# Layer 0 of a four-layer convolution and attention network: a written order for its convolutions, one tile of x kept in SBUF, batch norms of q, k and v apart, attention's first image begun earlier

## The chip, the cores and the metric

The kernel runs on one core of a Trainium2 chip. The core has five engines with queues of their own: TensorE (PE, with its weight loads listed as PEld), VectorE (DVE), ScalarE (ACT), GpSimd (POOL) and SyncE (SP), which here only issues DMAs. The metric is the device time of one execution in microseconds (us), lower is better.

## The reference, cut to what matters

x has the shape (8, 384, 32, 32), float32. Four layers each add their output to x. The change lies in layer 0:

```python
def _dwproj(x, dw, g, b, pw):                     # for q, k and v, with weights of their own
    y = conv(x, dw, 3x3, padding 1, depthwise)    # 384 channels
    y = gelu(_bn(y, g, b))                        # batch norm over (image, h, w), per channel
    return einsum('oc,bchw->bohw', pw, y)
...
q, k, v = (_dwproj(gn(x), ...) per heads of 48 channels)
attn = softmax(einsum('bhcn,bhcm->bhnm', q, k) * scale)
out = einsum('oc,bchw->bohw', w_out, attn @ v)
x = x + _bn(out)
```

gn is a group norm of x per image (32 groups of 12 channels). The batch norm of q, say, needs the mean and variance of q's convolution over all eight images, so no gelu of q can run before all of q's convolutions are done. The other layers (a mixture of four experts, a 7x7 depthwise convolution, a fusion of three branches) aren't touched.

## The kernel before

The 384 channels are three tiles of 128 partitions, ct = 0, 1, 2; an image has N = 1024 pixels. Layer 0 has these stages.

**Statistics** (L237 to L246). Each image of x is loaded whole (1.5 MB, SP, L241, four buffers), DVE takes its statistics (bn_stats, L140, bn_aggr, L245), and `gn_coefs` turns these into a scale and a shift per channel and image (s0, t0).

**Inputs** (`prepare`, L252 to L264). For one ct, each image's 128 channels are loaded again (0.5 MB, SP, L259, tile xn, three buffers), normalized by ACT (`affine`, L200) and transposed in 32x32 blocks by DVE (L261) into xt0, where 32 channels x 32 rows lie so that a convolution along a row is a banded 32x32 matrix. xt0 has two buffers. POOL clears its border rows.

**Convolutions** (`convolve0`, L266 to L292). For each (ct, v), v = q, k, v, a block of four groups u. A group loads a weight tile (0.4 MB, on ACT's queue, L271, four buffers), runs 96 matmuls of the source, 192 in the trace, on 32x32 pieces of PE (L278) into one of two PSUM buffers of four banks, and ACT copies the buffer into the tile o (L284, two buffers of o). After four groups, DVE transposes each image back into y (L290, four buffers), takes the batch norm's statistics (L140), and SP writes y to DRAM (raw[v][b], L292). I call the last three the results of a block.

The order here is that of the source as a scheduler arranges it: `prepare(0)`, `prepare(1)`, the blocks (0, q), (0, k), (0, v), then `prepare(2)`, then the six others. After the last block `bn_coefs` (L203 to L210) computes scale and shift of all nine (v, ct) at once: bn_aggr on DVE, a power on POOL (L135), and three small products.

**Attention** (`attention(False)`). From here the order on PE, ACT and DVE is that of the source (`manual_schedule`); SP and POOL are arranged by the scheduler, in order of the source as a rule. For each image, `fetch` loads q, k and v (1.5 MB each, L364), `activate` applies batch norm and gelu on ACT (three affines of 128x1024, L200), `project_k` and `project_q` multiply by pw_k and pw_q (36 matmuls of the trace each, L380, into three PSUM buffers of two banks, evicted by ACT and by DVE copies, L398 and L400), `scores` multiplies q by k (L472) and takes exp on ACT (L479), `project_v` (L425) makes v, `attend` (L491) multiplies. For the first image the order is: fetch(0), gelu of k, gelu of q, project_k, gelu of v, project_q, scores, project_v. `attention(True)` is a second version that runs only if a sum left the range of float32; it is skipped with these inputs.

After the batch norms, and before attention in the source, w1 (2.3 MB, the experts' weights of layer 1), gate_w and gate_b are loaded on SP.

Of the kernel before, what the change touches and what calls it, by code (L numbers as in the profile page):

```python
# [17 lines left out]
P = 128  # L18
# [49 lines left out]
def img(a):  # L68
    return a.rearrange("p (h w) -> p h w", w=W)
# [3 lines left out]
def conv_mixer_kernel(ctx: ExitStack, tc: tile.TileContext, a: dict, out: bass.AP):  # L73
# [63 lines left out]
    def bn_stats_of(bs, src):  # L137

        for h in range(2):
            nc.vector.bn_stats(bs[:, h, :], src[:, h * HF : (h + 1) * HF])  # L140
# [58 lines left out]
    def affine(o, i, s, t, func=AF.Identity):  # L199
        nc.scalar.activation(o, i, func, bias=t, scale=s)  # L200

    def bn_coefs(stats, gb, n, s, t):

        mv = small.tile([P, 2, 9], FP, tag="bn_mv", name="bn_mv")
        for i in range(n):
            nc.vector.bn_aggr(mv[:, :, i], stats[:, i].rearrange("p a s -> p (a s)"))
        rsqrt(s, mv[:, 1, :n])
        nc.vector.tensor_mul(s, s, gb[:, :, 0])
        nc.vector.tensor_mul(t, mv[:, 0, :n], s)
        nc.vector.tensor_sub(t, gb[:, :, 1], t)  # L210
# [19 lines left out]
        for v in range(3)  # L230
    ]

    with tc.tile_pool(name="cw", bufs=1) as cw, tc.tile_pool(name="cxt", bufs=2) as cxt:
        bn_gb = load(cw, "bn_gb", nc.scalar)
        stats = cw.tile([P, 9, 2 * B, 6], FP, name="stats")
        with tc.tile_pool(name="cx", bufs=4) as cx, tc.tile_pool(
            name="cgn", bufs=2, space=PSUM  # L237
        ) as cgn:
            for b in range(B):
                x = cx.tile([P, NC, N], FP, tag="x", name="x")  # L240
                nc.sync.dma_start(out=x, in_=a["x"][b])  # L241
                for ct in range(NC):
                    bs = xst[:, ct, 2 * b : 2 * b + 2, :]
                    bn_stats_of(bs, x[:, ct, :])
                    nc.vector.bn_aggr(mvx[:, :, ct, b], bs.rearrange("p a s -> p (a s)"))  # L245
            s0, t0 = gn_coefs((mvx[:, 0], mvx[:, 1]), cgn)  # L246

        with tc.tile_pool(name="co", bufs=2, reuse_waits="tile") as co, tc.tile_pool(
            name="cy", bufs=3, reuse_waits="tile"
        ) as cy, tc.tile_pool(name="cps", bufs=2, space=PSUM, reuse_waits="tile") as cps:  # L250

            def prepare(ct):  # L252

                xt = cxt.tile([P, 32, B, H + 2], FP, tag="xt0", name="xt0")
                for row in (0, H + 1):
                    nc.gpsimd.memset(xt[:, :, :, row : row + 1], 0.0)
                for b in range(B):
                    xn = cy.tile([P, N], FP, tag="xn", name="xn")
                    nc.sync.dma_start(out=xn, in_=a["x"][b, :, ct, :])  # L259
                    affine(xn, xn, s0[:, ct, b : b + 1], t0[:, ct, b : b + 1])  # L260
                    nc.vector.transpose(  # L261
                        xt[:, :, b, 1 : 1 + H].rearrange("p c h -> p h c"), img(xn)
                    )
                return xt  # L264

            def convolve0(ct, v, xt):  # L266

                o = co.tile([P, B, H, 32], FP, tag="o", name="o")
                for u in range(4):
                    w = cy.tile([P, 2, 4, 3, W], FP, tag="w", name="w", bufs=4)  # L270
                    nc.scalar.dma_start(out=w, in_=a["w0"][ct, v, u])  # L271
                    ps = cps.tile([P, 4, 2, B, H], FP, tag="ps", name="ps")
                    for cc in range(2):
                        for k in range(3):
                            for j in range(4):
                                for i in range(4):
                                    r = slice(32 * i, 32 * i + 32)
                                    nc.tensor.matmul(  # L278
                                        ps[32 * j : 32 * j + 32, i, cc],
                                        lhsT=w[r, cc, j, k, :],  # L280
                                        rhs=xt[r, 8 * j + 2 * u + cc, :, k : k + H],
                                        start=k == 0, stop=k == 2,
                                    )
                    nc.scalar.copy(  # L284
                        o.rearrange("p b h (i c) -> p i c (b h)", i=4)[:, :, 2 * u : 2 * u + 2],
                        ps.rearrange("p i c b h -> p i c (b h)"),
                    )
                for b in range(B):
                    y = cy.tile([P, N], FP, tag="y", name="y", bufs=4)
                    nc.vector.transpose(img(y), o[:, b])  # L290
                    bn_stats_of(stats[:, v * NC + ct, 2 * b : 2 * b + 2, :], y)
                    nc.sync.dma_start(out=raw[v][b][:, ct, :], in_=y)  # L292

            xts = [prepare(0), prepare(1)]
            for ct in range(NC):
                for v in range(3):
                    convolve0(ct, v, xts[ct])
                    if (ct, v) == (0, 2):
                        xts.append(prepare(2))
        bn_coefs(stats, bn_gb, 9, bn_s, bn_t)  # L300


    zraw = [dram.tile([P, NC, N], FP, tag=f"z{b}", name=f"z{b}") for b in range(B)]
    wpool = ExitStack()
    wp = wpool.enter_context(tc.tile_pool(name="wp", bufs=1))
    w1 = load(wp, "w1")
    gate_w = load(wp, "gate_w")
    gate_b = load(wp, "gate_b")
    zpool = ExitStack()
    zs = zpool.enter_context(tc.tile_pool(name="zs", bufs=1))  # L310
    zst = zs.tile([P, NC, 2 * B, 6], FP, name="zst")
# [6 lines left out]
    def attention(shifted):  # L318
# [3 lines left out]
        with tc.tile_pool(name="aw", reuse_waits="tile", bufs=1) as aw, tc.tile_pool(  # L322
# [5 lines left out]
            w_out = load(aw, "w_out")  # L328
            if shifted:

                pw_q, pw_k = load(aw, "pw_qs"), load(aw, "pw_ks")
                ones_row = aw.tile([P, 1], FP, name="ones_row")
                nc.gpsimd.memset(ones_row, 0.0)
                nc.gpsimd.memset(ones_row[0:1, :], 1.0)
                nc.gpsimd.memset(ones_row[64:65, :], 1.0)
            else:
                pw_q, pw_k = load(aw, "pw_q"), load(aw, "pw_k")

                own = aw.tile([P, 3], FP, name="own")
                nc.gpsimd.memset(own, 1.0)
                for o, base, sign in ((1, 15, -1), (2, -16, 1)):
                    for q in range(4):
                        v = own[32 * q : 32 * q + 32, o : o + 1]
                        nc.gpsimd.affine_select(
                            out=v, in_=v, compare_op=ALU.is_ge, fill=0.0, base=base,
                            pattern=[[0, 1]], channel_multiplier=sign,
                        )
                nc.gpsimd.tensor_copy(own[32:64, 0:1], own[32:64, 1:2])  # L350
                nc.gpsimd.tensor_copy(own[64:96, 0:1], own[64:96, 2:3])
# [1 line left out]
            nc.gpsimd.memset(vT, 1.0)  # L353
            chk = aw.tile([P, B * 2 * NP], FP, name="chk")
            if shifted:
                mx = aw.tile([P, 4, P], FP, name="mx")
                nc.gpsimd.memset(mx, 0.0)
            ys, kTs, qTs, atts, xs = {}, {}, {}, {}, {}

            def fetch(b):  # L360
                ys[b] = []
                for v in range(3):
                    y = ay.tile([P, NC, N], FP, tag=f"y{v}", name=f"y{v}", bufs=1)
                    nc.sync.dma_start(out=y, in_=raw[v][b])  # L364
                    ys[b].append(y)

# [181 lines left out]
            ]  # L548
            per_b = len(todo) // B
            fetch(0)  # L550
            activate(0, 1)
            last = None
            for i, t in enumerate(todo):
                b, j = t[0], i % per_b
                if j == 0:
                    activate(b, 0)
                    project_k(b)
                    activate(b, 2)
                    project_q(b)
                    if shifted:  # L560
                        shift(b)
                es = scores(*t)
                complete = attend(*last) if last else None
                if j == 0:
                    project_v(b)
                    if b + 1 < B:
                        fetch(b + 1)
                if complete:
                    complete()
                last = (*t, es)  # L570
                if j == 3 and b > 0:
                    project_out(b - 1, 1)
                if j == per_b // 2 + 3:
                    if b + 1 < B:
                        activate(b + 1, 1)
                    project_out(b, 0)
# [10 lines left out]
                nc.vector.tensor_scalar(shift_needed, ps[:1, :1], P - 0.5, None, ALU.is_lt)  # L587
            project_out(B - 1, 1)

    ORDERED = {mybir.EngineType.PE, mybir.EngineType.Activation, mybir.EngineType.DVE}  # L590
    with tc.manual_schedule(engines=ORDERED):
        attention(False)
    redo = nc.values_load(shift_needed[:1, :1], min_val=0, max_val=1)
    with tc.If(redo > 0):
        attention(True)
# [2 lines left out]
    with tc.tile_pool(name="mg", bufs=2, space=PSUM) as mg:  # L598
# [32 lines left out]
        v.tensor_copy(s1, s)  # L631
        v.tensor_copy(t1, t)
    zpool.close()


    r2mem = [dram.tile([P, B, N], FP, tag=f"r2_{ct}", name=f"r2_{ct}") for ct in range(NC)]
# [1107 lines left out]
```

## Time and profile before

| | us |
|---|---|
| median of 3 runs (3489.36 to 3500.19) | 3489.73 |
| the profiled execution's own time | 3488.85 |
| span of the profiled execution, first to last instruction | 3487.1 |

Where its time goes, from the timeline:

| stage | from | to |
|---|---|---|
| statistics of x, group norm coefficients | 0 | 54.4 |
| first affine of an input | 54.46 | |
| first convolution matmul | 74.37 | |
| last convolution matmul's end | 333.9 | |
| last eviction of a convolution | 333.96 | 337.53 |
| last results, batch norm coefficients | 337.57 | 359.6 |
| loads of q, k, v of image 0 issued | 360.93 | |
| first gelu (after its table load at 376.51) | 377.80 | |
| projections of k and q | 379.09 | 413.1 |
| attention's scores, first to last image, and the rest of it | 413.09 | about 1846 |
| layer 1 | about 1846 | about 2940 |
| layers 2 and 3 | about 2940 | 3487 |

The profile is one execution, recorded by the hardware. A group of it reads: line of the kernel, engine, operation, output <- inputs, how many (xN), then busy time, mean duration, and the idle time of the engine just ahead of it with what ended that idle time. Where a trace shows nothing that the engine waited for, it says "issue". PEld is the loading of weights, beside the matmuls. The granted clock is the share of its full clock that TensorE was given.

Four more rows that a reader can use: in the convolutions each block has 19.2 us of work on DVE (eight results), 15.0 us on ACT (four evictions) and about 18 to 20 us of busy PE; from the first eviction of a block to that of the next it takes some 28 us; the 16 DMA engines are busy 60% of the time. Between 337.5 and 376.5 PE is idle (granted clock 0.50), DVE is busy 19.9 us, and the DMA engines 81%.

### The profile page before, as it was taken

The numbers are of one execution on the slowest core, as the hardware profiler recorded it, in microseconds if no ns is written. First come the engines' busy times: TensorE is split into PE (matmuls) and PEld (weight loads), VectorE is DVE, ScalarE is ACT, GpSimd is POOL, SyncE is SP. The second block draws the span as 40 slices with busy tenths as digits, with TensorE's granted clock in tenths as the row PEclk, the third lists the DMA queues.
The fourth block names the chain that finished last, engine by engine and source line by source line (L and its number), as shares of the span: only waits on it lengthen the run. The fifth ranks groups of instructions, "written<-read, shape, count | busy, mean of one in ns | idle before, by whom it ended". The sixth has DMA issues, their size and how long they took to land. (4 is left out here: it accounts for less than half of the span.)

```text
span 3487.1 us, 56144 instructions
## 1 busy us (share of the span) xinstructions
PE 3086.0 (88%) x24960; PEld 1407.2 (40%) x24960; DVE 1600.9 (46%) x2185; ACT 1204.4 (35%) x1147; POOL 139.9 (4%) x318
## 2 busy tenths in 40 slices
PE   2655699999999999999997999999999998565889
PEld 2443234343333333333433444444444444444444
DVE  6677344444444444444443464343243331546164
ACT  2654254544545353535343402122122111213320
POOL 1000000000000000000000000000000000110100
PEclk9888799999999999999998999999999998886889
DMA  6655401111111111110006422122021002556656
GB/s 257 221 209 213 154 20 58 38 55 41 55 41 55 39 39 57 39 57 21 21 21 226 136 72 100 33 76 78 16 78 64 22 29 104 186 175 206 222 191 205
DMA packets 97250, 342.68 MB, mean 98 GB/s; under 512 B 13984, under 2 KB 16776, under 8 KB 92456
## 3 DMA queue, kind: packets, MB, share of 16 engines
q1 hardware_dynamic: 81816, 290.01, 23.9%
q0 software_dynamic: 9184, 32.49, 2.6%
q10 hardware_dynamic: 6000, 16.53, 1.5%
q8 instruction: 197, 3.23, 0.4%
q14 instruction: 53, 0.43, 0.0%
HBM read 240.58 MB, written 101.53 MB: 98 GB/s over the span
## 5 line engine op out<-in xcount | busy, mean ns | idle before, releaser
L479 ACT ACTIVATE e<-sc 128x1024 f32<-128x1024 f32 x512 | 484.2, 1030 | 580.5 <-PE sc L472 580.2
L681 PE MATMUL ph<-xn,w 128*128 128x512 f32 x1152 | 525.0, 594 | 0.5 <-ACT xn L200 0.5
L894 PE MATMUL y<-hs,w 128*128 128x512 f32 x1152 | 519.8, 593 | 1.2 <-DVE hs L879 1.1
L472 PE MATMUL sc<-qT,kT 64*128 64x512 f32 x2048 | 478.8, 604 | 20.7 <-DVE qT L398 15.4
L491 PE MATMUL av<-e,vT 128*64 128x512 f32 x2048 | 468.5, 599 | 0.0
L685 ACT ACTIVATE hs<-ph,b 128x512 f32<-128x512 f32 x192 | 131.6, 685 | 630.3 <-PE ph L681 628.7
L894 PEld LDWEIGHTS y<-hs,w 128*128 128x128 f32 x1152 | 217.9, 190 | 273.9 <-issue 263.7
L681 PEld LDWEIGHTS ph<-xn,w 128*128 128x128 f32 x1152 | 216.3, 190 | 268.4 <-issue 258.5
L472 PEld LDWEIGHTS sc<-qT,kT 64*128 64x128 f32 x2048 | 186.1, 186 | 307.3 <-issue 229.4
L879 DVE TENSOR_TENSOR hs<-hs,cb 128x512 f32<-128x512 f32 x192 | 130.9, 691 | 358.2 <-ACT hs L685 351.3
L278 PE MATMUL ps<-xt,w 32*32 32x256 f32 x6912 | 167.7, 432 | 116.5 <-issue 90.8
L491 PEld LDWEIGHTS av<-e,vT 128*64 128x64 f32 x2048 | 135.8, 137 | 317.7 <-issue 317.7
L507 DVE RECIPROCAL inv<-sm 128x512 f32<-128x512 f32 x64 | 214.6, 3353 | 2.2
L1213 PE MATMUL ps<-xt,w 32*32 32x256 f32 x5376 | 138.2, 448 | 75.5 <-POOL w L974 37.6
L505 DVE LOAD_MASK_SELECT sm<-av x64 | 0.9, 14 | 417.1 <-PE av L491 417.1
L278 PEld LDWEIGHTS ps<-xt,w 32*32 32x32 f32 x6912 | 114.2, 109 | 169.3 <-issue 117.3
L884 DVE SCALAR_TENSOR_TENSOR r<-cb,b,r 128x512 f32<-128x512 f32 x192 | 135.0, 746 | 87.5 <-DMA cb<-cfmem 86.0
L380 PE MATMUL sc<-y,pw_k 128*128 128x512 f32 x288 | 128.6, 606 | 45.2 <-ACT y L200 45.2
L284 ACT COPY o<-ps 128x2048 f32<-128x2048 f32 x36 | 134.1, 3741 | 82.9 <-PE ps L278 82.9
L1213 PEld LDWEIGHTS ps<-xt,w 32*32 32x32 f32 x5376 | 94.9, 111 | 117.6 <-issue 51.2
L1158 ACT COPY o<-ps 128x2048 f32<-128x2048 f32 x20 | 73.8, 3689 | 170.3 <-PE ps L1213 136.1
L530 PE MATMUL sc<-att,w_out 128*128 128x512 f32 x288 | 129.3, 604 | 0.2 <-DMA att<-att 0.2
(284 smaller groups left out, 2771.0 us busy)
## 6 DMA issues: line engine op xcount, KB each, us to landing
raw<-y SPq DMA_DIRECT2D x72, 512.0 KB
y<-raw SPq DMA_DIRECT2D x24, 1536.0 KB
xr<-in_x SPq DMA_DIRECT2D x42, 512.0 KB
cb<-cfmem SPq DMA_DIRECT2D x64, 256.0 KB
w<-in_w ACTq DMA_DIRECT2D x36, 384.0 KB
w<-in_w SPq DMA_DIRECT2D x24, 532.0 KB
x<-in_x SPq DMA_DIRECT2D x8, 1536.0 KB
xn<-in_x SPq DMA_DIRECT2D x24, 512.0 KB
```

The lines of the kernel that those rows point to most:

```text
L278: nc.tensor.matmul(ps[32 * j : 32 * j + 32, i, cc], lhsT=w[r, cc, j, k, :], rhs=xt[r, 8 * j + 2 * u + cc, :, k : k + H], start=k == 0, sto ...
L284: nc.scalar.copy(o.rearrange("p b h (i c) -> p i c (b h)", i=4)[:, :, 2 * u : 2 * u + 2], ps.rearrange("p i c b h -> p i c (b h)"),)
L472: nc.tensor.matmul(sc[:, s, :], lhsT=kTs[b][r, pair, m * P : (m + 1) * P], rhs=qTs[b][r, pair, h * HF : (h + 1) * HF], start=True, stop=True,)
L479: nc.scalar.activation(e, sc, AF.Exp, scale=1.0 if shifted else HD**-0.5)
L491: nc.tensor.matmul(av[64 * s : 64 * s + 64, :], lhsT=vT[:, m, c0 : c0 + 64], rhs=e[:, s, :], start=m == 0, stop=m == N // P - 1,)
L507: nc.vector.reciprocal(inv, sm)
L681: nc.tensor.matmul(ph, lhsT=w1[:, e, ct, dc * P : (dc + 1) * P], rhs=xn[:, ct, :], start=ct == 0, stop=ct == NC - 1,)
L685: nc.scalar.activation(hs, ph, AF.Relu, bias=b1[:, e, dc : dc + 1])
L879: nc.vector.tensor_mul(hs, hs, cb[e])
L884: nc.vector.scalar_tensor_tensor(out=out[oc], in0=cb[e], scalar=b2[:, oc, e : e + 1], in1=out[oc], op0=ALU.mult, op1=ALU.add,)
L894: nc.tensor.matmul(py[oc], lhsT=w2[:, e, dc, oc * P : (oc + 1) * P], rhs=hs, start=k == 0, stop=k == len(TODO) - 1,)
L1213: nc.tensor.matmul(ps[32 * j : 32 * j + 32, i, c % 2], lhsT=w[r, j, k, :W], rhs=xts[ct][r, 8 * j + c, :, k : k + H], start=k == 0, stop=k ...
```

## The change

It does these things:

1. **Tile 0 of x is kept.** The first 128 channels of each image are loaded by a DMA of their own into x0, which lies in a buffer of o; the other 256 channels go into x as before. The statistics read both. The inputs of ct 0 are made from x0 in place, with no second load.
2. **A written order.** All of layer 0 up to the last batch norm is in `manual_schedule` for PE, ACT and DVE. Nine blocks m = 0 to 8 run as 36 groups. After the matmuls of a group stand, in this order: the load of the weights three groups ahead, the inputs that this group makes (block 0: two images of ct 1 in each group; blocks 3 to 5: one or two images of ct 2 in the first two groups), some results of the block before (1, 2, 2 and 3 images in the four groups), and the eviction.
3. **Buffers of the inputs.** ct 0 and ct 2 share one buffer of xt0 (pool cxa); ct 1 has one on the right side of SBUF (pool cxb), given back after block 5. Its place goes to a pool pre0 that holds pw_q and pw_k (loaded then, on SP) and attention's tiles y0 and y1 (q and k).
4. **Batch norms apart.** `coefs0(v)` computes the coefficients of q after block 7, of k after block 8, of v at the end, three columns each.
5. **The first image sooner.** After the coefficients of q and of k their first image is fetched, and gelu is applied on ACT: q's after group 1 of the last block, k's after its last eviction. In attention the first image then begins with project_k, and v's gelu stands behind project_q.
6. **Other places.** w1, gate_w and gate_b are loaded after attention in the source; the second version of attention uses pre0 for two of its tiles.

The core of the diff:

```diff
-            xts = [prepare(0), prepare(1)]
-            for ct in range(NC):
-                for v in range(3):
-                    convolve0(ct, v, xts[ct])
-                    if (ct, v) == (0, 2):
-                        xts.append(prepare(2))
-        bn_coefs(stats, bn_gb, 9, bn_s, bn_t)
+        x0 = co.tile([P, B, H, 32], FP, tag="o", name="o").rearrange("p b h c -> p b (h c)")
...
+                x = cx.tile([P, NC - 1, N], FP, tag="x", name="x")
+                nc.sync.dma_start(out=x0[:, b], in_=a["x"][b, :, 0])
+                nc.sync.dma_start(out=x, in_=a["x"][b, :, 1:])
...
+                if ct == 0:
+                    xn = x0[:, b]
+                else:
+                    xn = cy.tile([P, N], FP, tag="xn", name="xn")
+                    nc.sync.dma_start(out=xn, in_=a["x"][b, :, ct, :])
+                affine(xn, xn, s0[:, ct, b : b + 1], t0[:, ct, b : b + 1])
...
+            for n in range(3):
+                weights_of(n)
+            for b in range(B):
+                prepare0(0, b)
+            for n, (ct, v, u) in enumerate(groups):
...
+                weights_of(n + 3)
+                m = n // 4
+                if m == 0:
+                    for b in (2 * u, 2 * u + 1):
+                        prepare0(1, b)
+                if m in (3, 4, 5) and u < 2:
+                    for b in ((0, 1), (2,), (3, 4), (5,), (6, 7), ())[2 * (m - 3) + u]:
+                        prepare0(2, b)
+                if (m, u) == (5, 3):
+                    cxb_pool.close()
...
+                    for i, k in enumerate("qk"):
+                        nc.sync.dma_start(out=pw[:, i], in_=a[f"pw_{k}"])
+                if m > 0:
+                    for b in ((0,), (1, 2), (3, 4), (5, 6, 7))[u]:
+                        results(*last, b, last_o)
+                nc.scalar.copy(
...
+                if u == 3:
+                    last, last_o = (ct, v), o
+                    if ct == NC - 1 and v > 0:
+                        coefs0(v - 1)
+                        y0 = pp0.tile([P, NC, N], FP, tag=f"y{v - 1}", name="y0")
+                        nc.sync.dma_start(out=y0, in_=raw[v - 1][0])
+                        ys0[v - 1] = y0
+                if m == 8 and u in (1, 3):
+                    gelu0(u // 2)
+            for b in range(B):
+                results(*last, b, last_o)
+            coefs0(2)
...
                 if j == 0:
-                    activate(b, 0)
+                    begun = b == 0 and not shifted
+                    if not begun:
+                        activate(b, 0)
                     project_k(b)
-                    activate(b, 2)
+                    if not begun:
+                        activate(b, 2)
                     project_q(b)
+                    if begun:
+                        activate(b, 2)
```

`results` and `weights_of` hold the lines of `convolve0` that they are named for; `coefs0(v)` calls `bn_coefs` for three columns, `gelu0(v)` three affines with gelu.

## The prediction
> **What bounds the kernel now.** I read the list of cores first (one core, span 3487.1 us, mean granted TensorE clock 0.951), then the page's 40 slices, then the busy times by stretch, the waits of each engine between 60 and 420 us, and the timeline of layer 0. Behind layer 0 TensorE sets the pace: it is busy 1370 of 1396 us from 438 to 1834 (attention) and 1065 of 1094 us from 1846 to 2940. The change touches nothing there but two weight tiles' places, so a microsecond by which attention begins sooner should be a microsecond at the end. In layer 0 TensorE is not full. Two groups of the page, of the 32x32 convolution and of its eviction:
>
> ```profile
> L278 PE MATMUL ps<-xt,w 32*32 32x256 f32 x6912 | 167.7, 432 | 116.5 <-issue 90.8
> L284 ACT COPY o<-ps 128x2048 f32<-128x2048 f32 x36 | 134.1, 3741 | 82.9 <-PE ps L278 82.9
> ```
>
> The matmuls take 167.7 us of a stage that runs from 74.4 to 337.5. What PE waits for, and then ACT, from 60 to 420 us (total, times, longest):
>
> ```profile
> PE ps L278 <- issue: 90.8, 43, 24.7
> PE sc L380 <- ACT y L200: 45.2, 1, 45.2
> PE ps L278 <- ACT o L284: 25.5, 4, 12.5
> ...
> ACT L200 <- DMA y<-raw: 39.0, 1, 39.0
> ACT xn L200 <- DMA xn<-in_x: 34.0, 16, 10.5
> ```
>
> So three things: 45.2 us once, before attention's first projection; 25.5 us behind evictions that ACT ran late; and 90.8 us of "issue", of which 24.7 is the wait before the first matmul. The rest of "issue" has a cadence: in the timeline of PE from 200 to 230 us, chunks of 128 matmuls stand 4 to 5 us apart (205.20, 209.86, 215.23, 219.82, 223.94), each 2.7 to 4.0 us long with 1.3 to 2.6 us of idle between. In the DMA view of 200 to 335 us the instruction queue moves 29 packets, 0.48 MB, 16.5 KB each, while PE runs 3788 matmuls and 3772 weight loads: 261 instructions a packet, 128 matmuls and their loads. I read that as PE waiting for its own instructions. An order of work does not change it, so I leave it in the sum.
>
> [...]
>
> The end of the stage, from the timeline (start, duration, engine, line; idle before and releaser in brackets):
>
> ```profile
> 333.96 3.57 ACT L284 COPY o<-ps 128x2048 f32<-128x2048 f32 x1 [3.92 <-PE ps L278]
> ...
> 360.93 1.90 SPq L364 DMA_DIRECT2D y<-raw  x3
> ...
> 376.51 1.28 ACT L200 ACT_TABLE_LOAD   x1 [38.97 <-DMA y<-raw]
> ...
> 379.09 18.61 PE L380 MATMUL sc<-y,pw_k 128*128 128x512 f32 x36 [45.18 <-ACT y L200]
> ```
>
> Last eviction, 18.6 us of results on DVE (337.57 to 356.2), 3.4 us of coefficients (to 359.6), 17 us for the fetch, then gelu and PE. The reader is to see a serial chain of 45 us with PE idle.
>
> **Start.** Before, ct 0's eight images are loaded a second time, and ACT waits for these loads. Kept in SBUF, they cost no load: from 54.46 (when the group-norm coefficients are there) one affine of 1.24 us, then eight transposes back to back, 5.35/3 = 1.78 us each: 70.0. PE starts at 70.2 instead of 74.37: -4.2 us. The statistics before that: DVE waits 2.9 us for images 1 to 3 (0.62, 1.17, 1.10) while 4 weight tiles (1.5 MB) share the queues from 0.8 us on. The first tile of each image now lands by itself, and the weights sit in buffers that x uses first, so I take -2 us; bounds -5 (the waits and the late first image) and +1 (SP issues 16 loads, not 8, about 0.65 us each, mostly beside the transfers).
>
> **Convolutions.** A block is four groups of 192 matmuls. From eviction to eviction the nine blocks take 37.2, 22.6, 28.4, 38.8, 24.4, 28.4, 27.7, 27.8, 27.9, sum 263.2 us (busy times by stretch). Block 0 holds a 10.8 us wait for an eviction that stood on ACT behind ct 1's inputs, block 3 one of 12.5 us behind ct 2's:
>
> ```profile
> 95.69 6.38 PE L278 MATMUL ps<-xt,w 32*32 32x256 f32 x192 [10.81 <-ACT o L284]
> ...
> 197.82 2.76 PE L278 MATMUL ps<-xt,w 32*32 32x256 f32 x67 [12.54 <-ACT o L284]
> ```
>
> In the new order each group carries at most two inputs: ACT 2 x 1.24 + 3.74 = 6.2 us beside PE's 6.5 to 7, DVE 2 x 1.9 + at most three results of 2.3 = 10.7 in one group but 19.2 + 5.7 of 27.7 in a block. Both hide under PE. The weights are issued three groups ahead, into a buffer whose matmuls ACT's last eviction has already waited for. The wait added on SP is the load of pw_q and pw_k, which needs PE to leave ct 1's input; three raw writes queue behind it, and four y buffers let DVE go on until the block ends: nothing. Cover gone, each input left on ACT's path is 1.24 us. Block 0 then takes 26.8 (37.2 less 10.4, the 10.8 being partly a prefilled start), the others 27.7, the row most blocks lie at: 26.8 + 8 x 27.7 = 248.4, -14.8 us. Ends: all at 24.4, 222 (-41); all at 28.4, 255.6 (-7.6).
>
> **Tail.** T is the end of the last convolution matmul (333.9 before). Before, relative to T: k projection +45.2, first score +79.2, first exp +81.7 (415.62), v projection +85.0 (418.92). After: q's and k's batch norms are separate, q's gelu lies in the last block (3 x 1.16 + 1.28 table load, on ACT under PE), and k's results are done 19 us into that block, so its 1.5 MB fetch (15.6 us for 5.25 MB at 361 to 376 makes 4.5) is in before the last eviction. Eviction to +3.6, gelu to +4.8, k projection +4.8 to about +21. DVE meanwhile does v's results, to +22.2, and coefficients, to +25.6; only then the k copies (7 x 1.22, releasing the three PSUM tiles at +28.1, +31.8, +34.2). So q's three projections of 5.2 us run from +28.1 to +43.7, first score +44.5. ACT: last q eviction +44.9, v's gelu, now behind q, 3.5 us to +48.4, table load 1.28, first exp +49.7; v projection about +52.5. That is -32.5 us at the v projection, from where the order is the old one. What is late next is DVE's results, not the fetch. y of v (1.5 MB) is issued after the last raw write, +24, and is needed at +44.9: hidden by 15 us. Bounds: -36 (at the scores) and -17 (rival 1).
>
> PE rests 7 us between k and q. In the rows, k's projection after 39 us at granted clock 0.50 took 18.61 and q's at full clock 15.61, so this is at most +3; I take 0 in the sum, as q is paced by three releases. [...]
>
> **Other edits.** w1 (2.3 MB) is now issued after attention's last SP load (1796) and needed at 1873: nothing; were it issued behind the branch it would cost up to 7 us at the 15.6 us for 5.25 MB rate. Weight tiles that move between pools: nothing.
>
> **Sum.** -4.2 - 2 - 14.8 - 32.5 = -53.5 us. The profiled execution took 3488.85 (span 3487.1), 0.9 under the median 3489.73; from the median, 3436.
>
> **Rivals.**
> 1. k late: the fetch of k's first image stands on SP behind v's raw writes, or k's PSUM or kT tile is not free before v's results are done. Then fetch at +22.2, in at +28, projection +29.5, 31.2 us for k and q, scores about +62: -17 instead of -32.5: 3452. For: SP is in order and not in the written list. Against: in program order the fetch stands ahead of v's results. 0.17.
> 2. The blocks gain nothing (new waits, raw writes meeting the instruction loads): 3436 + 14.8 = 3451; at 28.4 each, 3443. For: blocks 4 and 1 were faster than the rest, perhaps in exchange for the stall before. 0.14.
> 3. The blocks run like block 4, 24.4: 3410. 0.07.
> 4. First image not earlier at all (all of attention's first tiles wait for v's buffers): only -21: 3469. 0.05.
> 5. Slower: in the written order an ACT affine whose load is late blocks the eviction behind it, and through two PSUM buffers PE. Place: 16 inputs of ct 1 and ct 2. At the longest such wait of before, 10.5 us, 168 us: 3604; it decides from 53.5/16 = 3.3 us exposed an image, and 6 us would give 3532. Against: the mean such wait was 2.1 us (34.0/16), three buffers are loaded ahead, and a group has about half a microsecond on ACT and a whole PSUM buffer of slack. 0.05, a fifth of it about no change.
>
> **The numbers.** The forecast has 0.52, 3424 to 3448 by itself. The range 3415 to 3460 takes rivals 1 and 2 in and leaves 3, 4 and 5 out. A measurement here can tell 0.3%, about 10.5 us, from no change: faster 0.95, within 0.01, slower 0.04.
>
> **What would show it.** First matmul near 68 to 70; no PE wait for evictions of over 3 us in the convolutions; the chunks of 128 at the same 4 to 5 us; last convolution matmul near 313 to 317; one gelu table load before it; k projection within 6 us and v projection within 55 of it. Wrong if PE waits for ACT behind "DMA xn<-in_x", or if the y fetch lands after v's results.

## The result, and the profile after

The changed kernel takes 3453.52 us (median of 4, 3440.27 to 3459.79) against 3491.2 for the kernel before (median of 4): a ratio of 0.9882, 95% interval 0.9848 to 0.9916. A later measurement of the same two gave 3450.39 against 3492.92, 0.9885 (0.9866 to 0.9903). So 38 and 43 us were gained; the forecast was 53.5 us, 3436, in a range of 3415 to 3460. The profiled execution took 3453.2 us, its span is 3451.5.

Two groups of the page after, the convolutions and the projections of k and q:

```profile
L449 PE MATMUL sc<-y,pw 128*128 128x512 f32 x576 | 254.1, 602 | 12.0 <-DVE kT L467 7.3
L325 PE MATMUL ps<-xt,w 32*32 32x256 f32 x6912 | 161.9, 418 | 106.8 <-issue 106.8
```

All of PE's idle time in front of convolution matmuls is "issue" now. What PE waits for from 55 to 420 us, and one line of what ACT waits for:

```profile
PE ps L325 <- issue: 106.8, 50, 20.3
PE sc L449 <- DVE kT L467: 7.3, 1, 7.3
PE sc L449 <- ACT y L200: 4.7, 1, 4.7
...
ACT kT L200 <- DVE y L295: 15.4, 1, 15.4
```

The waits for evictions (25.5 us) are gone, and of the 45.2 us ahead of the projections 4.7 are left. In their place stand 7.3 us for k's copies on DVE, and more "issue". Without the wait ahead of the first convolution matmul (24.7 and 20.3 us) "issue" in the convolutions was 66.1 us before and is 86.5 now, 20.4 more: most of the 25.5 us came back as "issue". PE's busy time there went from 167.7 to 161.9 us.

The start, from the timeline. First DVE's first statistics, before and then after (the second line of each is the next wait for a load):

```profile
8.84 1.88 DVE L140 BATCH_NORM_STATS2 xst<-x 128x6 f32<-128x512 f32 x3 [8.84 <-DMA x<-in_x]
...
13.50 1.88 DVE L140 BATCH_NORM_STATS2 xst<-x 128x6 f32<-128x512 f32 x3 [0.62 <-DMA x<-in_x]
```

```profile
4.90 1.29 DVE L140 BATCH_NORM_STATS2 xst<-o 128x6 f32<-128x512 f32 x2 [4.90 <-DMA o<-in_x]
...
7.39 1.29 DVE L140 BATCH_NORM_STATS2 xst<-x 128x6 f32<-128x512 f32 x2 [0.95 <-DMA x<-in_x]
```

Then ACT's first affine, the eight transposes and the first matmuls, after:

```profile
50.00 1.24 ACT L200 ACTIVATE o<-o,gn_t,gn_s 128x1024 f32<-128x1024 f32 x1 [37.59 <-DVE gn_t L185]
...
51.27 14.06 DVE L280 STREAM_TRANSPOSE xt<-o 128x1024 f32<-128x1024 f32 x8 [1.31 <-ACT o L200]
...
65.54 7.45 PE L325 MATMUL ps<-xt,w 32*32 32x256 f32 x293 [20.31 <-issue]
```

The statistics end 4.5 us sooner (50.00 against 54.46), and the transposes run without a gap. The tail, from the last eviction on:

```profile
313.98 3.63 ACT L350 COPY o<-ps 128x2048 f32<-128x2048 f32 x1 [0.86 <-PE ps L325]
...
317.41 3.48 ACT L200 ACTIVATE y<-y,bn_t,bn_s 128x1024 f32<-128x1024 f32 x3
...
318.69 17.26 PE L449 MATMUL sc<-y,pw 128*128 128x512 f32 x36 [4.75 <-ACT y L200]
...
340.63 8.66 DVE L467 COPY kT<-sc 32x1024 f32<-32x1024 f32 x7
...
343.22 18.62 PE L449 MATMUL sc<-y,pw 128*128 128x512 f32 x36 [7.28 <-DVE kT L467]
...
370.78 16.84 PE L494 MATMUL sc<-pw_v,y 128*128 128x384 f32 x48
```

k's gelu follows the last eviction at once, and k's projection (the first L449 line) starts 4.8 us behind the last convolution matmul. Then DVE is late: its copies of k begin at 340.63, when the results and coefficients of v are done, and q's projection waits for them.

Where the 35.6 us between the two profiled executions come from, stage by stage:

| stage | before | after | difference |
|---|---|---|---|
| span's start to the first convolution matmul | 74.4 | 65.5 | -8.8 |
| convolutions, to the end of the last matmul | 259.5 | 248.4 | -11.1 |
| from there to the first v projection | 85.0 | 56.8 | -28.2 |
| from there to the first 7x7 matmul (attention, layer 1) | 2507.1 | 2511.6 | +4.4 |
| from there to the end (layers 2 and 3) | 561.1 | 569.1 | +8.1 |

At the first v projection the changed kernel is 48 us ahead, at the end 36.

### The profile page after: what moved, and what is told of

It is laid out like the page before. It is cut to its first block, busy times and chain, and to the rows that moved or that the text cites. A ratio compares the mean times of both kernels' runs of the same rounds, so it can differ in the third digit from the quotient of the medians.

```text
span 3451.5 us, 56137 instructions
## 1 busy us (share of the span) xinstructions
PE 3085.5 (89%) x24960; PEld 1403.8 (41%) x24960; DVE 1610.4 (47%) x2193; ACT 1202.3 (35%) x1147; POOL 140.8 (4%) x320
## 5 line engine op out<-in xcount | busy, mean ns | idle before, releaser
L541 PE MATMUL sc<-qT,kT 64*128 64x512 f32 x2048 | 481.7, 607 | 22.1 <-DVE qT L467 15.4
L449 PE MATMUL sc<-y,pw 128*128 128x512 f32 x576 | 254.1, 602 | 12.0 <-DVE kT L467 7.3
L325 PE MATMUL ps<-xt,w 32*32 32x256 f32 x6912 | 161.9, 418 | 106.8 <-issue 106.8
L1291 PE MATMUL ps<-xt,w 32*32 32x256 f32 x5376 | 135.2, 438 | 82.4 <-POOL w L1052 39.6
L325 PEld LDWEIGHTS ps<-xt,w 32*32 32x32 f32 x6912 | 109.8, 107 | 158.5 <-issue 136.3
L449 PEld LDWEIGHTS sc<-y,pw 128*128 128x128 f32 x576 | 110.4, 193 | 155.2 <-issue 147.2
L1291 PEld LDWEIGHTS ps<-xt,w 32*32 32x32 f32 x5376 | 91.9, 110 | 124.5 <-issue 56.9
```

The costliest lines, as they stand in the source:

```text
L325: nc.tensor.matmul(ps[32 * j : 32 * j + 32, i, cc], lhsT=w[r, cc, j, k, :], rhs=xt0s[ct][r, 8 * j + 2 * u + cc, :, k : k + H], start=k == ...
L449: nc.tensor.matmul(ps[:, h, :], lhsT=w[:, ct, pair, :], rhs=y[:, ct, h * HF : (h + 1) * HF], start=ct == 0, stop=ct == NC - 1,)
L541: nc.tensor.matmul(sc[:, s, :], lhsT=kTs[b][r, pair, m * P : (m + 1) * P], rhs=qTs[b][r, pair, h * HF : (h + 1) * HF], start=True, stop=True,)
L1291: nc.tensor.matmul(ps[32 * j : 32 * j + 32, i, c % 2], lhsT=w[r, j, k, :W], rhs=xts[ct][r, 8 * j + c, :, k : k + H], start=k == 0, stop=k ...
```

## The experiments

Each is the changed kernel with one edit, if nothing else is said. "Stage" below is the time from the first to the last convolution matmul's start; "tail" is the time from the last convolution matmul's end to the first v projection. All profiles in one table, with the medians where they were timed:

| kernel | stage | tail | layers 2, 3 | time (runs) |
|---|---|---|---|---|
| before, four profiles | 259, 252, 254, 253 | 85, 85, 85, 84 | 561, 568, 567, 558 | 3488 to 3493 (4 to 11) |
| after, two profiles | 248, 243 | 57, 56 | 569, 572 | 3453.5 (4), 3450.4 (6) |
| e2_no_early | 261 | 55 | 570 | 3467.1 (4) |
| e3_reload0 | 243 | 56 | 571 | 3453.1 (4) |
| e5_half_columns | 234 | 56 | 564 | 3432.1 (1) |
| e6_w_once | 237 | 57 | 570 | 3442.1 (1) |
| e7_k_on_act | 242 | 48 | 576 | 3443.1 (4) |
| e8_one_norm | 250 | 71 | 564 | 3461.5 (6) |
| e9_lumped | 256 | 55 | 571 | 3458.7 (6) |
| e10_tail_undone | 238 | 79 | 566 | 3459.5 (4) |

### e1_after_again, e4_before_again, e11_before_third, e12_before_fourth

No edit. They ask what of the differences is the change's and what comes and goes.

> The changed kernel once more. In its first profile the change was 48 us ahead of the kernel before at attention's first v projection and 36 us ahead at the end; 8 of the 12 us went in layers 2 and 3 (first 7x7 convolution matmul to the end: 569.1 us, before 561.0). Theory A: layers 2 and 3 vary by themselves, and the change has no part in it; then this stretch differs from 569 by some us here, and the two kernels' stretches overlap. Theory B: the change costs 8 us there (places of tiles, code); then it stays near 569. Time under both: 3440 to 3460.

> The kernel before once more, for a second profile. Theory A (layers 2 and 3 vary by themselves): first 7x7 matmul to the end differs from 561 by some us. Theory B: 561 again, within 1 us. Time 3489 to 3500.

> The kernel before, for a third profile. First 7x7 matmul to the end: 561.0 and 568.2 us so far, 564.5 to 576 in eight profiles with the change (mean 570). Theory A (the stretch varies by itself): 561 to 576, and the means of four and eight profiles are not apart by more than their scatter. Theory B (the change costs there): 561 to 568 again. Convolution stage 252 to 260 under both.

> The kernel before, for a fourth profile; as for e11_before_third.

The same program varies: the stage of the kernel before by 7 us (252 to 259), of the changed one by 5, and layers 2 and 3 by 10 (558 to 568 before). The first profile of before had the longest stage of the four. On the means of four and two profiles the stage is 254.4 and 245.6, so 8.8 us gained and not 11.1: the waits for evictions fell by 24.4 us, "issue" rose by 17.9, and PE's busy time fell by 2.3. Layers 2 and 3 have a mean of 563.6 in four profiles of before and 569.3 in ten with the change and its variants (564 to 576). That is 6 us with ranges that overlap: neither theory is settled by it.

### e3_reload0: the kept tile

```diff
-                if ct == 0:
-                    xn = x0[:, b]
-                else:
-                    xn = cy.tile([P, N], FP, tag="xn", name="xn")
-                    nc.sync.dma_start(out=xn, in_=a["x"][b, :, ct, :])
+                xn = cy.tile([P, N], FP, tag="xn", name="xn")
+                nc.sync.dma_start(out=xn, in_=a["x"][b, :, ct, :])
```

> The changed kernel, but the inputs of ct 0 are loaded again as before (x0 still feeds the statistics). Theory: of the 8.8 us by which the first convolution matmul came sooner (74.4 to 65.5), 4.4 are the kept tile (ACT no longer waits for loads) and 4.4 the earlier statistics (weights out of the way of x); so first matmul 65.5 + 4.4 = 70, time +4, 3457. Rival: with the statistics done 4 us sooner the first three loads are also in sooner and the rest keep pace: first matmul 66 to 67, time +1.

Measured: 3453.08 (ratio to before 0.9901, 0.9865 to 0.9937), and in the profile:

```profile
68.64 1.24 ACT L200 ACTIVATE xn<-xn,gn_t,gn_s 128x1024 f32<-128x1024 f32 x1 [1.32 <-DMA xn<-in_x]
69.47 7.71 PE L322 MATMUL ps<-xt,w 32*32 32x256 f32 x293 [24.51 <-issue]
```

The first matmul comes at 69.5, 3.9 us later, as the theory has it, and ACT waits for loads again. In the time the 4 us can't be told from the scatter. The other half of the earlier start stays: it is the earlier statistics. In these the first data is there at 4.90 us instead of 8.84, and DVE then waits 0.95 us instead of 2.9. Two edits can do that, the first tile's own small load and the weights, three of whose loads are issued at 26.8 us instead of four at 0.8; no run tells the two apart.

### e9_lumped: the order of the inputs

```diff
-                if m == 0:
-                    for b in (2 * u, 2 * u + 1):
-                        prepare0(1, b)
-                if m in (3, 4, 5) and u < 2:
-                    for b in ((0, 1), (2,), (3, 4), (5,), (6, 7), ())[2 * (m - 3) + u]:
-                        prepare0(2, b)
+                if m in (0, 3) and u == 0:
+                    for b in range(B):
+                        prepare0(1 if m == 0 else 2, b)
```

> The changed kernel with its written order, but all eight inputs of ct 1 are made in group 0 of block 0 and all of ct 2 in group 0 of block 3, ahead of that group's eviction. Theory: the two waits for evictions come back, about 10.8 and 12.5 us on PE, of which 11 to 16 us remain at the end of the convolutions (259.5 before, 248.4 after); time 3465. Rival: PE waits for instructions anyway and makes the stalls good (block 4 took 24.4 after the stall): less than 5 us.

Measured: 3458.73 (0.9915, 0.9891 to 0.9940), stage 256. What PE waits for:

```profile
PE ps L325 <- issue: 86.4, 45, 20.3
PE ps L325 <- ACT o L347: 23.5, 2, 14.8
```

The two waits for evictions are back, 23.5 us, and "issue" falls by 12 to 20 against the two profiles after (106.8, 98.7). In the profile of before PE ran 284 matmuls, more than two chunks, in 7.06 us without a stop behind its wait of 12.54 us. So of 23.5 us of removed waits about 10 are a gain (256.3 against 245.6), under the theory's 11 to 16 and over the rival's 5, and the rest turns into "issue". That is one profile against two, and the stage of one program varies by 5 to 7. The lump alone brings the stage of the written order into the range of before (252 to 259).

### e5_half_columns: what paces the convolutions

Taps 1 and 2 are computed for four of the eight images only, so the convolution is not the reference's.

```diff
-                                    ps[32 * j : 32 * j + 32, i, cc],
+                                    ps[32 * j : 32 * j + 32, i, cc, : B if k == 0 else B // 2],
                                     lhsT=w[r, cc, j, k, :],
-                                    rhs=xt0s[ct][r, 8 * j + 2 * u + cc, :, k : k + H],
+                                    rhs=xt0s[ct][
+                                        r, 8 * j + 2 * u + cc, : B if k == 0 else B // 2, k : k + H
+                                    ],
```

> The changed kernel with as many matmuls, but taps 1 and 2 only over four of the eight images (the other four get tap 0 alone): two thirds of the columns. Theory (PE waits for its own instructions in the convolutions): the chunks of 128 stay 4 to 5 us apart, the stage of 248 us (first matmul to last) loses less than 25. Rival (PE's own work or its clock sets the pace): 2.75 us a chunk become 1.9, the stage loses 54 chunks x 0.9 = 49 us or more, until DVE's 19.2 us a block and ACT's 15 bind at about 180.

Measured: stage 234 us, 12 less than the mean after; a third of the columns is gone. PE's timeline:

```profile
202.93 2.32 PE L325 MATMUL ps<-xt,w 32*32 32x256 f32 x128 [0.49 <-issue]
207.20 2.18 PE L325 MATMUL ps<-xt,w 32*32 32x128 f32 x128 [1.96 <-issue]
211.57 3.10 PE L325 MATMUL ps<-xt,w 32*32 32x128 f32 x127 [2.19 <-issue]
```

The chunks of 128 are shorter and still 4.3 us apart. By itself this does not refute the rival. PE's busy time in the stage fell by 16 us only (147.3 against 161.9 and 164.8) and not by 49, as the matmuls shortened less than their columns and the granted clock was lower (0.82 against 0.92 and 0.90), and the stage lost 12 of these 16.

What settles it are the DMA records of the traces. In the stage after, the instruction queue moves 54 packets of 16,384 bytes while PE runs 13,824 matmuls and weight loads; that makes 256 a packet. Five packets and the chunks that follow them, from the changed kernel's first profile (us):

| packet landed | chunk of 128 started |
|---|---|
| 255.63 | 256.99 |
| 259.82 | 261.27 |
| 264.76 | 266.14 |
| 273.02 | 274.41 |
| 278.78 | 280.06 |

So it goes in all fourteen profiles: 626 times PE stood still for over 0.4 us in the convolutions with "issue" as the cause, and each time it went on 0.6 to 1.6 us, in the middle 1.4, after such a packet had landed. In the changed kernel's first profile these are 48 stops of 86.1 us together, each of which ended 1.2 to 1.6 us after a landing. I read that as PE waiting for its instructions.

### e6_w_once: does data hold up the instructions?

Only the first four weight tiles are loaded, and all 36 groups use them, so the convolutions have wrong weights.

```diff
                 if n < len(groups):
-                    w = cy.tile([P, 2, 4, 3, W], FP, tag="w", name="w", bufs=4)
-                    nc.scalar.dma_start(out=w, in_=a["w0"][groups[n]])
-                    weights0[n] = w
+                    if n < 4:
+                        w = cy.tile([P, 2, 4, 3, W], FP, tag="w", name="w", bufs=4)
+                        nc.scalar.dma_start(out=w, in_=a["w0"][groups[n]])
+                        weights0[n] = w
...
-                w = weights0.pop(n)
+                w = weights0[n % 4]
```

> The changed kernel with only the first four weight tiles of the convolutions loaded and used for all 36 groups (32 of 36 loads of 384 KB left out, 12.6 MB of the stage's some 55 MB). Theory: PE's instruction loads wait behind data in the DMA engines (5 to 8 us between loads while y or raw moves, 3.5 to 4 when it is quiet), so less data shortens the stage, 246 us on the mean of three profiles, by 8 to 15. Rival: the fetch has a fixed pace and the data has no part in it: 241 to 250 as in the changed kernel.

Measured: stage 237 us, 8.5 below the mean of 245.6 and 5 below the lowest of the four profiles that share the changed kernel's convolutions and fetches (248, 243, 242, 250). That is the theory's lower end. It is one profile, and the fetches of image 0 are still in it.

### e10_tail_undone and e8_one_norm: what the tail's parts are worth

e8 computes all nine columns at the end and takes the old order of gelus and projections; e10 also puts q's and k's tiles back into attention's pool.

```diff
-                    if ct == NC - 1 and v > 0:
-                        coefs0(v - 1)
-                        y0 = pp0.tile([P, NC, N], FP, tag=f"y{v - 1}", name="y0")
-                        nc.sync.dma_start(out=y0, in_=raw[v - 1][0])
-                        ys0[v - 1] = y0
-                if m == 8 and u in (1, 3):
-                    gelu0(u // 2)
...
-            coefs0(2)
+            bn_coefs(stats, bn_gb, 9, bn_s, bn_t)
...
-            if shifted:
-                activate(0, 1)
+            activate(0, 1)
...
-                    begun = b == 0 and not shifted
+                    begun = False
```

and in e10 alone

```diff
-                    pool = pp0 if v < 2 else ay
-                    y = pool.tile([P, NC, N], FP, tag=f"y{v}", name=f"y{v}", bufs=1)
+                    y = ay.tile([P, NC, N], FP, tag=f"y{v}", name=f"y{v}", bufs=1)
```

> The changed kernel with one batch norm of all nine columns at the end and the old order of gelus and projections for image 0; q's and k's fetch may still go early, as their tiles are free. Theory: DVE's 25.6 us after the last convolution matmul come first, then gelu of k, k's and q's projections with no gap: first v projection 68 us after the last convolution matmul (57 in the changed kernel, 85 before): time +11, 3464, so the apart batch norms are worth 11 us and the early fetch 17. Rival: the early fetch is worth nothing by itself: 85 us, 3481.

> One batch norm at the end and the old order of gelus and projections, as in e8_one_norm, and image 0's tiles of q and k back in attention's own pool, so that their fetch waits for the convolutions' buffers; only w1 still stands behind the fetches in the source. Theory: against e8_one_norm (first v projection 71.5 us after the last convolution matmul) the fetch is exposed again, 3 MB instead of the 5.25 MB of before: about 6 us, so 77 to 79, and 7 less than the 85.3 of before, which is w1's share. Time 3468. Rival: the order of the fetches alone decides and w1 had no share: 85, 3475.

Measured: e8 3461.49 (0.9929, 0.9901 to 0.9957), tail 71; e10 3459.49 (0.9921, 0.9904 to 0.9937), tail 79. What PE waits for ahead of the first projection, in e8 and then in e10:

```profile
PE sc L442 <- ACT y L200: 31.6, 1, 31.6
```

```profile
PE sc L441 <- ACT y L200: 39.2, 1, 39.2
```

In the tail the order is as expected: 85 before, 79 with w1 behind the fetches, 71 with the fetches early, 57 with the batch norms apart (6, 8 and 14 us, each from one profile or two). But e10 is no slower than e8. Its stage takes 238 us, 8 less than the mean after and 12 less than e8's: what the early fetch gives in the tail it seems to take in the convolutions. The changed kernel's timeline around k's fetch shows how:

```profile
295.82 2.75 PE L325 MATMUL ps<-xt,w 32*32 32x256 f32 x128 [1.23 <-issue]
296.69 0.32 SPq L359 DMA_DIRECT2D y<-raw  x1
...
299.47 2.76 PE L325 MATMUL ps<-xt,w 32*32 32x256 f32 x128 [0.90 <-issue]
...
307.04 6.90 PE L325 MATMUL ps<-xt,w 32*32 32x256 f32 x236 [4.81 <-issue]
```

and the same part of the stage in e10, without a fetch:

```profile
289.32 2.75 PE L325 MATMUL ps<-xt,w 32*32 32x256 f32 x128 [1.50 <-issue]
292.97 2.75 PE L325 MATMUL ps<-xt,w 32*32 32x256 f32 x128 [0.91 <-issue]
296.70 2.81 PE L325 MATMUL ps<-xt,w 32*32 32x256 f32 x127 [0.97 <-issue]
```

Behind each 1.5 MB fetch one chunk comes 7.6 to 8.6 us after the one before it instead of 4 (q's fetch near 264 us, k's near 297; both profiles after have both gaps, e3 and e8 the gap at q's alone). The DMA records show what goes with it. Between 264.8 and 272.0 us, with q's fetch and three raw writes in the queues, the 16 DMA engines are 95% busy and no instruction packet moves; the next one starts at 272.06 and, once started, takes 0.96 us as others do. Two such gaps, some 4 us each, are as large as the 8 us. The 8 us themselves are one profile's, in a stage that varies by 5 to 7.

### e2_no_early: an undoing that did something else

```diff
-                        y0 = pp0.tile([P, NC, N], FP, tag=f"y{v - 1}", name="y0")
-                        nc.sync.dma_start(out=y0, in_=raw[v - 1][0])
-                        ys0[v - 1] = y0
...
-                if m == 8 and u in (1, 3):
-                    gelu0(u // 2)
...
-            if shifted:
-                activate(0, 1)
+            activate(0, 1)
...
-                    begun = b == 0 and not shifted
+                    begun = False
```

> The changed kernel with attention's first image begun as before: q, k and v fetched and activated after the last coefficients. Theory (the sum by stages): this gives back the tail, so first v projection 85 us after the last convolution matmul instead of 57, and 28 us more in all: 3453 + 28 = 3481. Rival: the fetch of image 0 meets less traffic now (w1 stands behind it), so that the old order's fetch takes 6 us instead of 15.6: then only 18 us more, 3471.

Measured: 3467.1 (0.9927, 0.9904 to 0.9950), tail 55, stage 261. With the coefficients of q and k ready early, attention's gelus stand ahead of the last evictions on ACT. I read that as the scheduler's doing: the written orders of layer 0 and of attention are two, and nothing orders one behind the other.

```profile
315.18 2.37 ACT L200 ACTIVATE y<-y,bn_t,bn_s 128x1024 f32<-128x1024 f32 x2 [9.65 <-DVE bn_t L210]
317.45 3.55 ACT L350 COPY o<-ps 128x2048 f32<-128x2048 f32 x1
...
321.06 5.79 PE L325 MATMUL ps<-xt,w 32*32 32x256 f32 x192 [11.48 <-ACT o L350]
```

ACT waited for k's coefficients with an eviction behind it, and PE's last group of convolutions waited 11.5 us. It tells nothing of the early image; it shows what a gelu in the wrong place costs, and why gelu0 is written into the last block.

### e7_k_on_act: a faster version

For image 0, k's copies of 32 partitions run on ACT, and kT is allocated first, so that it doesn't lie where the last block's o is.

```diff
+                        if first:
+                            nc.scalar.copy(d, ps[p : p + 32, :])
-                        if own is None or i is None:
+                        elif own is None or i is None:
...
-                    return spread(pw_k, ys[b][1], kT, None)
+                    return spread(pw_k, ys[b][1], kT, None, b == 0)
...
+            if not shifted:
+                kTs[0] = ay.tile([P, NP, N], FP, tag="kT", name="kT", bufs=1)
             fetch(0)
```

> The changed kernel with two more edits for image 0: k's seven copies of 32 partitions run on ACT instead of DVE, and the tile kT lies where the last block's o isn't. Theory: DVE's results are what is late in the tail (q's projection waits 7.3 us for k's copies, ACT 15.4 us for o); then q follows k with no gap, first v projection 47 us after the last convolution matmul instead of 57, and the time is 10 us lower, 3443. Rival: v's coefficients and its gelu, or v's fetch, are late next: first v projection at 52 to 57, 0 to 5 us lower.

Measured: 3443.11 (median of 4, 3439.30 to 3447.14; ratio to before 0.9860, 0.9837 to 0.9882), beside 3450.39 of the changed kernel on the same chip: 7 us less. All four runs are under all six of the changed kernel there (3448.76 to 3460.14).

```profile
312.50 33.93 PE L449 MATMUL sc<-y,pw 128*128 128x512 f32 x72 [4.75 <-ACT y L200]
...
346.36 1.99 PE L545 MATMUL sc<-qT,kT 64*128 64x512 f32 x8
...
355.36 6.92 PE L498 MATMUL sc<-pw_v,y 128*128 128x384 f32 x15
```

The 72 matmuls of k and q run without a gap, 33.93 us where the changed kernel takes 43.2 (318.69 to 361.84). The tail is 48 us. DVE's results were what was late.

## Why the prediction was right, and where it wasn't

The direction and the range were right, and the way in the main; the gain was 38 and 43 us and not 53.5. Of the signs named beforehand, the waits for evictions are gone, the last convolution matmul starts at 313.6 (308.7 in the second profile; 313 to 317 was said), k's projection is 4.8 us behind it, and one gelu table load stands before it. The first matmul came earlier than said (65.5 against 68 to 70), and the v projection 56.8 us behind the last convolution matmul and not within 55.

**Start** (-6.2 forecast): -8.8 in the profile. The kept tile gives what its row said (4.2 forecast; 3.9 in e3). The statistics were mis-sized: -2 forecast, -4.5 measured.

**Convolutions** (-14.8 forecast): the profile has -11.1, the means of several profiles -8.8. The mechanism was right: no wait for evictions is left, and e9 brings both back. Nor was the price of 27.7 us a block wrong on the mean. From the first matmul to the end of the last eviction the nine blocks were put at 248.4 us, and the two profiles have 252.1 and 247.3. What was mis-sized is mostly the stage before: the sum started from 263.2 us, of a profile that came out long, where the three others of the same kernel have 256.4 to 257.6.

That the price held is partly luck. Single blocks take 24.2 to 30.9 us. The fetch of image 0 was put in the last two blocks at no cost, but behind each of its 1.5 MB loads a chunk came 7.6 to 8.6 us after the one before instead of 4; without it the nine blocks take 241.7 us (e10, one profile). By that profile the blocks alone were priced too high, and the fetch at nothing, and the two nearly cancel. And the forecast took the cadence as one that an order of work doesn't change: 23.5 us of removed waits are worth about 10, as e9 shows, where "issue" was 12 to 20 us less beside these waits, and with 32 weight loads left out the stage was 8.5 us under the mean (e6, one profile).

Of the 248.4 us of the stage after, 86.5 are waits put down to "issue", nearly all of them in the 48 stops that end 1.2 to 1.6 us after an instruction packet has landed; in the second profile the waits are 78.4 of 243.6.

**Tail** (-32.5 forecast): -28.2, and -29 on the means. The serial order was right in each step: k's projection at +4.8, DVE's results and coefficients to +26.7 (25.6 forecast), then k's copies, then q. Mis-sized were the coefficients' end, by 1.1 us, and above all the 0 us for q's projection behind PE's rest of 7 us, by 3.0. q's projection took 18.62 us (17.13 in the second profile) where 15.6 was put from this line of before:

```profile
397.55 15.61 PE L380 MATMUL sc<-y,pw_q 128*128 128x512 f32 x36
```

The clock records of the traces account for it. The granted clock was 0.5 until 5.92 us into q's projection in the first profile, in a stretch of 10.24 us, and until 2.92 us in the second, in one of 6.83, and half of that, 2.96 and 1.46 us, is what q took more. The prediction had these 3.0 us as a bound and left them out of its sum. v's projection, behind the tail's end, took 16.84 us instead of 15.75 for the same reason (0.5 in its first 2.25 us). A second cause stands in the way without costing: ACT could not write kT before DVE was done with o (15.4 us), which I read as the two sharing memory; the copies on DVE were later anyway. e7 removes both.

The prediction's own arithmetic has two small slips here. From 79.2 to 44.5 us the first score gains 34.7 us, not the 36 of its bound, and the first exp at 49.7 with the 3.3 us from there to the v projection of before makes 53.0, not 52.5. Its idle times between chunks, "1.3 to 2.6 us", are 1.3 to 1.9 in that timeline.

**Other edits** (0 forecast): w1 moved in the source but not far in time. The prediction had it issued after 1796 us; it is issued at 340.6, still in the tail. Behind the fetches it no longer delays them, and e10 puts that at 6 us where the fetches are late, which the prediction had inside the tail's sum without naming it.

**Behind attention's start** (0 forecast, "a microsecond at the end"): the profiled pair lost 12.5 us there. Up to the 7x7 convolutions it is 4.4, of which the first image has 2.8 (176.2 against 173.4 us from v projection to v projection). But one of the four profiles of before has 2511.8 us in this stretch and 175.9 for the first image, so the kernels overlap there; the means are 2.7 us apart. Single stretches at a granted clock of 0.5 are part of such differences, 1.7 us for one of 3.41 us here. Two images of the changed kernel, one beside the other (columns: stretch, its length, PE, PEld, DVE, ACT, POOL, clock, DMA share, GB/s):

```profile
546.40:727.70 181.30, 178.62 (x670) 69.52 (x668) 84.50 (x102) 82.51 (x83) 4.65 (x8) 1.00 0.13 46
727.70:910.70 183.00, 180.33 (x670) 69.77 (x668) 84.50 (x102) 82.51 (x83) 4.64 (x8) 0.99 0.13 46
```

The same instructions take 1.7 us more at a clock of 0.99: the clock was 0.5 from 905.51 us on for 3.41 us. The profiles of before have such images too, one or two of seven. The 8.1 us in layers 2 and 3 are no more than what these layers vary by in one program (558 to 568); a cost of the change of some 6 us there is neither shown nor excluded, and its cause would be open. No experiment moved tiles or code to try it.

**The rivals**: rival 1 (k late behind v's raw writes) did not come; k's fetch stood where the source has it. Rival 2, that the blocks gain little because data meets the instruction loads, came true in part. Of rival 5 nothing was seen in the change itself; e2 shows its like, a gelu ahead of an eviction, at 11.5 us.

## What to carry to other kernels

Where PE runs many small matmuls, compare the spacing of its chunks with the packets of the instruction queue before you price a wait: a removed stall of 23.5 us gave about 10 here, as "issue" was 12 to 20 us more without it. Then a transfer that is "hidden" under such a stage may not be free: behind each of the two 1.5 MB fetches no instruction packet moved for some 7 us, with the DMA engines 95 and 91% busy. And take more than one profile of the kernel before as the base of a sum: here one stage of it varied by 7 us. When a wait goes, look at which engine is late next and at what it holds (here DVE with eight results in front of seven small copies), and give the small work to the engine that is idle.

## What the runs showed of the hardware

In the stage after there are 54 instruction packets of 16,384 bytes to 13,824 matmuls and weight loads, 256 a packet. 128 matmuls of 32x32 with 256 columns, and their loads, take PE 2.75 us at a granted clock of 1.0, but the load of a packet starts mostly 3.2 to 5 us after that of the last (39 and 38 of 53 times in the two profiles after), 7.8 to 8.4 us after it when a 1.5 MB fetch was issued in between, and once, in the first profile, 7.95 us after it with no fetch and the DMA engines 94% busy. Each of the 48 stops of over 0.4 us in that profile's convolutions ended 1.2 to 1.6 us, in the middle 1.4, after a packet had landed. The granted clock is 1.0 or 0.5 in the traces of before and after, with nothing between; around the tail of the changed kernel it changed after 3.41, 6.83, 10.24 and 17.07 us. ACT copies of 32x1024 from PSUM take 1.01 us each (three in 3.03, e7), DVE's 1.24 (seven in 8.66). In e5, with half the columns in two thirds of the matmuls, the chunks of 128 start 4.3 us apart on the mean (234 us by 54).
